# L3 attention: one product of 256 columns for the turned exponentials of two heads

## The chip, the cores and the metric

The kernel runs on one core of one Trainium2 chip. The metric is the time of one execution on the device in microseconds (us). Five engines work side by side, each through its own queue in order: TensorE (PE) multiplies matrices, VectorE (DVE) and ScalarE (ACT) read what PE leaves in PSUM, GpSimd (POOL) works on SBUF, and SyncE (SP) issues most of the transfers (DMA).

## The reference

The network has eight layers on 2048 tokens of 128 features, each of the form `x = layernorm(x + f(x))`: four pairs of an attention-like layer and a feed-forward layer, L0 to L3. The change touches only the attention of L3, which is this, cut to its core:

```python
NUM_HEADS, NUM_KV_HEADS, HEAD_DIM = 16, 4, 64
qkv = hidden_states @ qkv_w.T + qkv_b            # one sequence of 2048 tokens
xq, xk, xv = jnp.split(qkv, [H * D, H * D + KV * D], axis=-1)
xq = xq * scale                                  # scale from softplus(scaling), one per feature
xk = jnp.repeat(xk, 4, axis=2)                   # four query heads share one key head
xv = jnp.repeat(xv, 4, axis=2)
probs = jax.nn.softmax(jnp.einsum('bqhd,bkhd->bhqk', xq, xk))
out = jnp.einsum('bhqk,bkhd->bqhd', probs, xv)
return out.reshape(B, S, H * D) @ o_w.T + o_b
```

Every query sees all 2048 keys; there is no mask. All values are float32.

## The kernel before

Method `l3a` works on the attention of L3. The 2048 tokens are four blocks of 512 (`NB`), and each block is four tiles `t` of 128 queries. Of the four query heads of a key head `g`, two make a step: `groups` lists (block, tile, key head), each group gives two steps `s`, so there are 128 steps. The queries of a step's two heads are in the tile `qT` (64 features each), and a copy with the halves exchanged is in `qx`, made by two transfers of SP.

One of the two heads of a step goes the "A" way, the other the "B" way.

The A way has queries on the partitions. `scores_a(s, c)` (L1561) makes the scores of 128 queries against 1024 keys, in two halves c; DVE takes the maximum (`nm`, L1565), ACT the exponential with its sum (`e`, L1571); PE turns the result (`turn_a`, L1581), so that keys are on the partitions; ACT copies it out of PSUM (`et`, L1583); and `mixed_a` (L1593) multiplies it with the values `v`: 16 products of 128 columns, over 8 slices of keys in each of the two halves. A product's output has 64 partitions, so the two halves of the keys go side by side into the upper and the lower 64 partitions of `po`. ACT copies `po` to `pos` (L1602). Later the two halves are turned back (`divided`, L1630), scaled and added (`divided2`, L1635 and L1641), turned again (`turned`, L1645) and copied to `oA` (`turned2`, L1649).

The B way packs scores so that 32 queries lie on a quarter of the partitions and the four quarters hold four parts of the keys. `scores_b(s, x)` (L1677) makes them for two of the four groups of 32 queries at a time; DVE takes maxima (`st`, L1684), ACT exponentials (`eb`, L1692); statistics of the four parts are exchanged through DRAM by five transfers of SP (L1704, L1706) and joined (`joined1` to `joined3`, L1711 to L1729); POOL multiplies `eb` by the factors (L1732); DVE turns it in blocks of 32x32 (`turn_b`, L1739, `etb`); `mixed_b` (L1750) multiplies it with `v`, again 16 products of 128 columns; and DVE copies the result to `oB` (L1757).

At the end of each block, `out1` to `out5` multiply `oA` and `oB` with the output weights (L1763), add the input, normalize, and turn the result for the next layer.

The order on PE, DVE and ACT is written out by hand in `step(s)`; POOL's is left to the scheduler. A step computes scores and exponentials of `s + 1`, turns the A exponentials of `s`, and multiplies older ones with `v`: `mixed_a(s - 1)` in its first half, `mixed_b(s - 2)` in its second. `last(s)` closes it with the small products: queries for `s + 3` (L1537, `queries2` scales them on DVE, L1544), and one of `divided` and `turned`, in turn. Even and odd steps differ in these: one group is two steps, and what is made once per group (`factors1`, L1610, `factors3`, L1623, and the copy to `oA`) falls into one or the other.

What ties the engines together are few buffers. The scores and the turned A exponentials share the PSUM tile `s`, which has three buffers, taken in the order: A scores, turned A exponentials, B scores, and the same again in the second half of the step. `po` has one buffer, as has `tp`, which `last`, `out1`, `out2` and `out5` share:

```python
tc.tile_pool(name="l3a_s", bufs=3, space=PSUM) as ps,
tc.tile_pool(name="l3a_o", bufs=1, space=PSUM) as pso,
...
net.ps_t = shared.enter_context(tc.tile_pool(name=f"ps_t{len(net.coming)}", bufs=n, space=PSUM))
```

(`n` is 1 for `l3a`.)

Of the kernel before, what the change touches and what calls it, by code (L numbers as in the profile page):

```python
# [18 lines left out]
NB = NT // TB  # L19
NTILE = NT // 128  # L20
# [189 lines left out]
class _Net:  # L210
# [1254 lines left out]
    def l3a(self, xT, x_new):  # L1465
        nc, tc = self.nc, self.tc
        w = self.weights("w_l3a")
        wo = w[:, 1024:2560].rearrange("p (k m) -> p k m", k=12)
        rows = (slice(0, 64), slice(64, 128))
        with (  # L1470
# [14 lines left out]
            v = self.tile(one, [128, NTILE, 256], "v")  # L1485
            chunks = kT.rearrange("p x g (j m k) -> p x g j m k", m=NB, k=32)
            for b in range(NB):
                for g in (0, 1):
                    p = self.tile(ps, [128, 2, 512], "s")[:, 0, :]
                    nc.tensor.matmul(  # L1490
                        p,
                        lhsT=self.kv[:, g * 128 : (g + 1) * 128],
                        rhs=xT[:, b * TB : (b + 1) * TB],
                        start=True,
                        stop=True,
# [13 lines left out]
            oB = self.tile(one, [128, 8, 512], "oB")  # L1509
# [14 lines left out]
                    nc.vector.tensor_add(v[:, j, :], p[:, 0:256], self.bv)  # L1524


            groups = [(b, t, g) for b in range(NB) for t in range(4) for g in range(4)]
            n = 2 * len(groups)
            q_of, nm_of, den_of, e_of, et_of, po_of, pos_of, rec_of, ot_of, oT_of = ({} for _ in range(10))
            st_of, f_of, eb_of, etb_of, pob_of, r_of = ({} for _ in range(6))  # L1530

            def queries(s, p):

                b, t, g = groups[s // 2]
                c = 2 * g + s % 2
                at = b * TB + t * 128
                nc.tensor.matmul(  # L1537
                    p, lhsT=w[:, c * 128 : (c + 1) * 128], rhs=xT[:, at : at + 128], start=True, stop=True
                )
# [27 lines left out]

            def exponentials_a(s, c):
                k, h = divmod(s, 2)
                e = self.tile(sb, [128, 1024], "e", bufs=3)  # L1570
                nc.scalar.activation(  # L1571
                    e, e_of[s, c], AF.Exp, bias=nm_of[k][:, h, c : c + 1], accum_out=den_of[k][:, h, c : c + 1]
                )
                e_of[s, c] = e

            def turn_a(s, c):
                e = e_of.pop((s, c))
                tp = self.tile(ps, [128, 2, 512], "s").rearrange("p i (j q) -> p i j q", j=8)
                for j in range(8):
                    for i, r in enumerate(rows):  # L1580
                        nc.tensor.transpose(tp[:, i, j, :], e[r, j * 128 : (j + 1) * 128], self.ident[r, r])  # L1581
                et = self.tile(sb, [128, 2, 8, 64], f"et{c}", bufs=2 - c)
                nc.scalar.copy(et, tp)  # L1583
                et_of[s, c] = et

            def mixed_a(s):
                k, h = divmod(s, 2)
                g = groups[k][2]
                po = self.tile(pso, [128, 128], "po")
                ets = [et_of.pop((s, c)) for c in (0, 1)]  # L1590
                for j in range(8):
                    for c, r in enumerate(rows):
                        nc.tensor.matmul(  # L1593
                            po[r, :].rearrange("p (i q) -> p i q", i=2),
                            lhsT=v[:, 8 * c + j, g * 64 : (g + 1) * 64],
                            rhs=ets[c][:, :, j, :],
                            start=j == 0,
                            stop=j == 7,
                        )
                if h == 0:  # L1600
                    pos_of[k] = self.tile(sb, [128, 2, 128], "pos")
                nc.scalar.copy(pos_of[k][:, h, :], po)  # L1602


            wide = lambda x: x.unsqueeze(2).to_broadcast([128, 2, 2])
# [21 lines left out]
            def divided(k, tp):  # L1627
                pos = pos_of.pop(k)
                for h in range(2):
                    nc.tensor.transpose(tp[:, h, :], pos[:, h, :], self.ident)  # L1630
                ot_of[k] = tp
# [12 lines left out]
            def turned(k, tp):  # L1644
                nc.tensor.transpose(tp, ot_of.pop(k).rearrange("p h d -> p (h d)"), self.ident)  # L1645

            def turned2(k, tp):
                b, t, g = groups[k]
                nc.vector.tensor_copy(oA[:, g, t * 128 : (t + 1) * 128], tp)  # L1649

            def last(s):

                tp = self.tile(self.ps_t, [128, 4, 128], "tp")
                k, h = divmod(s - 2, 2)
                some = 0 <= k < len(groups)
                if some and h:
                    turned(k, tp[:, 1])
                if have(s + 3):
                    queries(s + 3, tp[:, 0])
                if some and not h:  # L1660
                    divided(k, tp[:, 1:3])
                if some and h:
                    turned2(k, tp[:, 1])
                if have(s + 3):
                    queries2(s + 3, tp[:, 0])
# [68 lines left out]
                    )  # L1734

            def turn_b(s, x):
                if x == 0:
                    etb_of[s] = self.tile(sb, [128, 4, 512], "etb")
                nc.vector.transpose(  # L1739
                    etb_of[s][:, 2 * x : 2 * x + 2, :].rearrange("p i k -> p (i k)"),  # L1740
                    eb_of.pop((s, x)).rearrange("p i k -> p (i k)"),
                )

            def mixed_b(s):
                b, t, g = groups[s // 2]
                po = self.tile(pso, [128, 128], "po")
                et = etb_of.pop(s)
                for j in range(NTILE):
                    r = rows[j % 2]
                    nc.tensor.matmul(  # L1750
                        po[r, :].rearrange("p (i q) -> p i q", i=4),
                        lhsT=v[:, j, g * 64 : (g + 1) * 64],
                        rhs=et[:, :, 32 * j : 32 * j + 32],
                        start=j < 2,
                        stop=j >= NTILE - 2,
                    )
                nc.vector.tensor_copy(oB[:, 2 * g + s % 2, t * 128 : (t + 1) * 128], po)  # L1757


            def out1(b):  # L1760
# [26 lines left out]
            have = lambda s: 0 <= s < n  # L1787

            def late(f, s, by, odd):

                k, h = divmod(s - by, 2)
                if h == odd and 0 <= k < len(groups):
                    f(k)

            def ends(f, s, by):

                if (s - by) % 32 == 31 and have(s - by):
                    f((s - by) // 32)

            def step(s):  # L1800
                new = have(s + 1)
                if new:
                    scores_a(s + 1, 0)
                if have(s):
                    turn_a(s, 0)
                if have(s - 1):
                    joined3(s - 1)
                late(factors1, s, 0, 1)
                if new:
                    exponentials_a(s + 1, 0)  # L1810
                    scores_b(s + 1, 0)
                ends(out1, s, 3)
                if s < 1:
                    values(range(8 * s + 8, 8 * s + 16))
                if new:
                    exponentials_b(s + 1, 0)
                if have(s - 2):
                    turn_b(s - 2, 1)
                late(divided2, s, 3, 0)
                if have(s - 1):  # L1820
                    mixed_a(s - 1)
                ends(out2, s, 4)
                if new:
                    scores_a(s + 1, 1)
                ends(out3, s, 4)
                if have(s):
                    turn_a(s, 1)
                late(factors2, s, 0, 1)
                if new:
                    exponentials_a(s + 1, 1)  # L1830
                    scores_b(s + 1, 1)
                late(factors3, s, 1, 1)
                if have(s):
                    joined1(s)
                if have(s - 1):
                    turn_b(s - 1, 0)
                ends(out4, s, 4)
                if new:
                    exponentials_b(s + 1, 1)
                if have(s):  # L1840
                    joined2(s)
                if have(s - 2):
                    mixed_b(s - 2)
                ends(out5, s, 4)
                last(s)

            with tc.manual_schedule(engines=MAIN - {mybir.EngineType.Pool}):
                keys_over(0)
                for s in (0, 1):
                    tp = self.tile(self.ps_t, [128, 4, 128], "tp")  # L1850
# [73 lines left out]
```

## Time and profile before

| what | value |
|---|---|
| three runs | 2726.64 us (median), 2713.97 to 2731.01 |
| the profiled execution | 2722.66 us, span 2720.8 us, mean granted TensorE clock 0.941 |
| busy: PE, DVE, ACT, POOL | 2446.3, 1801.6, 1481.7, 1165.3 us |
| first and last B-scores product (L1677) | start at 1258.9 and 2527.3 us |
| L1593 and L1750, PE | x4096 each, 276 ns mean, 252.0 and 251.9 us busy |
| L1739, DVE | x256, 1234 ns mean, 316.0 us busy |
| L1757, DVE | x128, 253 ns mean, 32.4 us busy |
| L1602, ACT | x128, 263 ns mean, 33.6 us busy |

The time of the run holds the span, from the first to the last instruction in the trace, and a little around it. Attention of L3 takes nearly half of the span. A float32 product shows as two matmul instructions, so 16 products are 32 of them (4096 = 128 x 32). Matmuls that follow each other overlap, so the mean of one (276 ns) is more than the time that it adds.

### The profile page before, as it was taken

Reading aid. Unit: us, or ns where it says so; the run is one execution under the profiler, and the core shown is the slowest. Engines: PE = TensorE matmul, PEld = TensorE weight load, DVE = VectorE, ACT = ScalarE, POOL = GpSimd, SP = SyncE. Lnnn points to the kernel's source line nnn. Section 1 sums busy time; section 2 is a strip of 40 time slices with the busy share of each in tenths; the row PEclk is TensorE's granted clock in tenths of the full one; section 3 lists DMA queues with packets and bytes.
Section 4 is the critical chain, followed back from the end, with each engine's and each line's share of the span. In section 5 each row is a group of like instructions: output and inputs, shape, how many; then the busy total and the mean of one; then the engine's idle time right before and its main releaser. Section 6 shows DMA issues by size and latency. Waiting matters only on the chain.

```text
span 2720.8 us, 59820 instructions
## 1 busy us (share of the span) xinstructions
PE 2446.3 (90%) x23773; PEld 1440.0 (53%) x23818; DVE 1801.6 (66%) x3156; ACT 1481.7 (54%) x2874; POOL 1165.3 (43%) x1403
## 2 busy tenths in 40 slices
PE   5779837998987888877999999999999999999998
PEld 3456524442224555543666656666566665666543
DVE  5443334013887777755888878888688887888311
ACT  1113312223435666644777757777577776777322
POOL 2142162003667776641555435554345553455200
PEclk8569957997998999998999999999999999999999
DMA  3011110000002111202000000000000000000000
GB/s 152 5 66 37 28 31 6 0 1 28 9 16 64 36 34 31 73 3 56 12 11 11 11 9 11 11 11 11 8 12 12 11 11 8 11 12 12 2 8 8
DMA packets 138923, 60.63 MB, mean 22 GB/s; under 512 B 100700, under 2 KB 130340, under 8 KB 137108
## 3 DMA queue, kind: packets, MB, share of 16 engines
q1 hardware_dynamic: 135942, 50.12, 8.0%
q0 software_dynamic: 2272, 4.66, 0.7%
q8 instruction: 190, 3.11, 0.5%
q10 hardware_dynamic: 432, 2.04, 0.2%
q14 instruction: 87, 0.70, 0.1%
HBM read 31.85 MB, written 5.23 MB: 14 GB/s over the span
## 4 chain that ended last, share of the span: by engine, by line
PE 76%; DVE 9%; ACT 6%; POOL 4%; issue 3%; DMA 1%; SPq 0%; POOLq 0%; DVEq 0%; ACTq 0%
PE s L1561 10%; PE s L1677 9%; PE po L1593 9%; PE po L1750 9%; PE mm L862 8%; PE s L1581 4%; PE h L673 3%; PE tp L1763 2%; PE tp L1537 1%; PE tp L703 1%; PE tp L1341 1%; DVE h L1068 1%; PE num L408 1%; PE mm L873 1%; PE mm L851 1%
## 5 line engine op out<-in xcount | busy, mean ns | idle before, releaser
L1732 POOL TENSOR_TENSOR eb<-eb,fb 128x1024 f32<-128x1024 f32 x256 | 479.5, 1894 | 5.0
L1583 ACT COPY et<-s 128x1024 f32<-128x1024 f32 x256 | 259.3, 1013 | 222.1 <-PE s L1581 221.9
L1692 ACT ACTIVATE eb<-s,st 128x512 f32<-128x512 f32 x512 | 347.0, 682 | 58.5 <-DVE st L1684 53.7
L1565 DVE TENSOR_REDUCE nm<-s 128x1 f32<-128x1024 f32 x256 | 313.3, 1224 | 87.1 <-PE s L1561 86.1
L1684 DVE TENSOR_REDUCE st<-s 128x2 f32<-128x1024 f32 x256 | 313.3, 1224 | 56.4 <-PE s L1677 49.5
L1739 DVE STREAM_TRANSPOSE etb<-eb 128x1024 f32<-128x1024 f32 x256 | 316.0, 1234 | 1.1 <-POOL eb L1732 0.9
L1561 PE MATMUL s<-kT,qx 64*128 64x512 f32 x512 | 290.9, 648 | 4.4 <-DMA qx<-qT 4.4
L1571 ACT ACTIVATE e<-s,nm 128x1024 f32<-128x1024 f32 x256 | 285.8, 1116 | 14.1 <-DVE nm L1565 13.7
L1561 PE MATMUL s<-kT,qT 64*128 64x512 f32 x512 | 290.0, 647 | 0.0
L1677 PE MATMUL s<-kT,qx 64*32 64x512 f32 x2048 | 279.2, 605 | 2.4 <-ACT eb L1692 2.4
L1677 PE MATMUL s<-kT,qT 64*32 64x512 f32 x2048 | 279.2, 605 | 0.0
L1593 PEld LDWEIGHTS po<-et,v 128*64 128x64 f32 x4096 | 221.1, 137 | 107.6 <-DVE db L1726 98.9
L1750 PEld LDWEIGHTS po<-etb,v 128*64 128x64 f32 x4096 | 221.0, 137 | 107.0 <-issue 106.3
L1750 PE MATMUL po<-etb,v 128*64 128x128 f32 x4096 | 251.9, 276 | 1.7 <-DVE etb L1739 1.3
L1593 PE MATMUL po<-et,v 128*64 128x128 f32 x4096 | 252.0, 276 | 0.7 <-DVE oB L1757 0.7
L1581 PEld LDWEIGHTS s<-ident,e 64*128 64x128 f32 x4096 | 170.2, 139 | 135.0 <-issue 103.8
L862 PE MATMUL mm<-h,wb 128*128 128x512 f32 x512 | 221.0, 592 | 0.0
L1581 PE MATMUL s<-ident,e 64*128 64x64 f32 x4096 | 169.8, 223 | 0.1
L297 POOL TENSOR_SCALAR ln_rs<-ln_mv 128x4 f32<-128x4 f32 x40 | 10.5, 262 | 365.8 <-DVE ln_mv L291 328.3
L875 DVE SCALAR_TENSOR_TENSOR r<-mm,vec,xT 128x512 f32<-128x512 f32 x8 | 6.0, 751 | 240.4 <-PE mm L873 240.4
L862 PEld LDWEIGHTS mm<-h,wb 128*128 128x128 f32 x512 | 97.3, 190 | 122.5 <-issue 119.8
L1729 POOL TENSOR_TENSOR fb<-dm,db 128x4 f32<-128x4 f32 x128 | 25.8, 202 | 259.6 <-DVE db L1727 132.8
(375 smaller groups left out, 4591.5 us busy)
## 6 DMA issues: line engine op xcount, KB each, us to landing
qx<-qT SPq DMA_DIRECT2D x256, 32.0 KB, 1.9
st<-std SPq DMA_DIRECT2D x512, 4.0 KB, 1.8
vo<-v SPq DMA_DIRECT2D x62, 128.0 KB, 2.4
ex<-in_w_ex_dram SPq DMA_DIRECT2D x4, 1536.0 KB, 16.9
rot<-in_rot_dram SPq DMA_DIRECT2D x32, 128.0 KB, 2.2
wb<-in_w_l1f_dram SPq DMA_DIRECT2D x1, 2816.0 KB, 9.5
wb<-in_w_l3f_dram SPq DMA_DIRECT2D x1, 2816.0 KB, 9.9
yd<-ys SPq DMA_DIRECT2D x39, 64.0 KB, 1.5
```

Source lines behind the costliest of these rows:

```text
L862: nc.tensor.matmul(p, lhsT=hid[i][:, k, c * 128 : (c + 1) * 128], rhs=h[:, k, :], start=k == 0, stop=k == 3,)
L1561: nc.tensor.matmul(p[:, i, :], lhsT=q_of[s][i][r, :], rhs=kT[r, (g + i) % 2, g // 2, at : at + 512], start=True, stop=True)
L1565: nc.vector.tensor_reduce(nm_of[k][:, h, c : c + 1], p, AX.X, ALU.max, negate=True)
L1571: nc.scalar.activation(e, e_of[s, c], AF.Exp, bias=nm_of[k][:, h, c : c + 1], accum_out=den_of[k][:, h, c : c + 1])
L1581: nc.tensor.transpose(tp[:, i, j, :], e[r, j * 128 : (j + 1) * 128], self.ident[r, r])
L1593: nc.tensor.matmul(po[r, :].rearrange("p (i q) -> p i q", i=2), lhsT=v[:, 8 * c + j, g * 64 : (g + 1) * 64], rhs=ets[c][:, :, j, :], start ...
L1677: nc.tensor.matmul(p[32 * m : 32 * m + 32, i, :], lhsT=q_of[s][1 - i][r, at : at + 32], rhs=chunks[r, (g + i) % 2, g // 2, :, m, :], start ...
L1684: nc.vector.tensor_reduce(st_of[s][:, 4, 2 * x : 2 * x + 2], p, AX.X, ALU.max, negate=True)
L1692: nc.scalar.activation(e[:, i, :], eb_of[s, x][:, i, :], AF.Exp, bias=st[:, 4, at : at + 1], accum_out=st[:, 4, 4 + at : 5 + at],)
L1732: nc.gpsimd.tensor_mul(e, e, f[:, 2 * x : 2 * x + 2].unsqueeze(2).to_broadcast([128, 2, 512]))
L1739: nc.vector.transpose(etb_of[s][:, 2 * x : 2 * x + 2, :].rearrange("p i k -> p (i k)"), eb_of.pop((s, x)).rearrange("p i k -> p (i k)"),)
L1750: nc.tensor.matmul(po[r, :].rearrange("p (i q) -> p i q", i=4), lhsT=v[:, j, g * 64 : (g + 1) * 64], rhs=et[:, :, 32 * j : 32 * j + 32], s ...
```

## The change

The A exponentials of step s and the B exponentials of step s - 1 are put into one tile `et` of shape [128, 2, 2, 4, 256]: half of the keys, A or B, group of 32 queries, and keys. `turn_a` writes its part in that order (PE's transposes now write two runs of 32 instead of one of 64, ACT's copy stays 1024 in a row), and `turn_b` writes the other part, in runs of 256. `mixed(s, part)` multiplies both with the same slice of `v` in one product of 256 columns, half of the 16 products in each half of the step. This needs both heads to belong to the same key head, so `groups` now runs over tiles inside of a key head; where the key head changes (15 times, and at both ends) `mixed` makes separate products of 128 columns as before. `copied` then copies both parts of `po` on ACT, at the end of the step: to `pos` and to `oB`. Both calls of `turn_b` for a step now stand together in the second half of the next one; before, one stood there and the other in the first half of the step after. `divided2`, and the work in `last` on the A part, come a step later; `out1` moves from the first half of its step to its end. The tile `e` has two buffers instead of three, `et` two of 16 KB per partition instead of the separate `et0`, `et1` and `etb`.

```diff
--- before.py
+++ after.py
@@ -1524,7 +1524,7 @@
                     nc.vector.tensor_add(v[:, j, :], p[:, 0:256], self.bv)
 
 
-            groups = [(b, t, g) for b in range(NB) for t in range(4) for g in range(4)]
+            groups = [(b, t, g) for b in range(NB) for g in range(4) for t in range(4)]
             n = 2 * len(groups)
             q_of, nm_of, den_of, e_of, et_of, po_of, pos_of, rec_of, ot_of, oT_of = ({} for _ in range(10))
             st_of, f_of, eb_of, etb_of, pob_of, r_of = ({} for _ in range(6))
@@ -1567,7 +1567,7 @@
 
             def exponentials_a(s, c):
                 k, h = divmod(s, 2)
-                e = self.tile(sb, [128, 1024], "e", bufs=3)
+                e = self.tile(sb, [128, 1024], "e")
                 nc.scalar.activation(
                     e, e_of[s, c], AF.Exp, bias=nm_of[k][:, h, c : c + 1], accum_out=den_of[k][:, h, c : c + 1]
                 )
@@ -1575,31 +1575,51 @@
 
             def turn_a(s, c):
                 e = e_of.pop((s, c))
-                tp = self.tile(ps, [128, 2, 512], "s").rearrange("p i (j q) -> p i j q", j=8)
+                tp = self.tile(ps, [128, 2, 512], "s").rearrange("p i (h j q) -> p i h j q", h=2, j=8)
                 for j in range(8):
                     for i, r in enumerate(rows):
-                        nc.tensor.transpose(tp[:, i, j, :], e[r, j * 128 : (j + 1) * 128], self.ident[r, r])
-                et = self.tile(sb, [128, 2, 8, 64], f"et{c}", bufs=2 - c)
-                nc.scalar.copy(et, tp)
-                et_of[s, c] = et
-
-            def mixed_a(s):
-                k, h = divmod(s, 2)
-                g = groups[k][2]
-                po = self.tile(pso, [128, 128], "po")
-                ets = [et_of.pop((s, c)) for c in (0, 1)]
-                for j in range(8):
+                        nc.tensor.transpose(tp[:, i, :, j, :], e[r, j * 128 : (j + 1) * 128], self.ident[r, r])
+                if c == 0:
+                    et_of[s] = self.tile(sb, [128, 2, 2, 4, 256], "et")
+                nc.scalar.copy(et_of[s][:, c, 0], tp.rearrange("p i h j q -> p (i h) (j q)"))
+
+            def mixed(s, part):
+
+                ga, gb = (groups[x // 2][2] if have(x) else None for x in (s, s - 1))
+                if part == 0:
+                    po_of[s] = self.tile(pso, [128, 8, 32], "po")
+                po, et = po_of[s], et_of[s]
+                if ga == gb:
+                    g, lo, hi, of = ga, 0, 8, range(4 * part, 4 * part + 4)
+                else:
+
+                    g, lo, hi, of = (gb, 4, 8, range(8)) if part else (ga, 0, 4, range(8))
+                if g is None:
+                    return
+                for j in of:
                     for c, r in enumerate(rows):
                         nc.tensor.matmul(
-                            po[r, :].rearrange("p (i q) -> p i q", i=2),
+                            po[r, lo:hi, :],
                             lhsT=v[:, 8 * c + j, g * 64 : (g + 1) * 64],
-                            rhs=ets[c][:, :, j, :],
+                            rhs=et[:, c].rearrange("p u i k -> p (u i) k")[:, lo:hi, 32 * j : 32 * j + 32],
                             start=j == 0,
                             stop=j == 7,
                         )
-                if h == 0:
-                    pos_of[k] = self.tile(sb, [128, 2, 128], "pos")
-                nc.scalar.copy(pos_of[k][:, h, :], po)
+
+            def copied(s):
+                po = po_of.pop(s)
+                et_of.pop(s)
+                if have(s):
+                    k, h = divmod(s, 2)
+                    if h == 0:
+                        pos_of[k] = self.tile(sb, [128, 2, 128], "pos")
+                    nc.scalar.copy(pos_of[k][:, h, :], po[:, 0:4, :].rearrange("p i q -> p (i q)"))
+                if have(s - 1):
+                    b, t, g = groups[(s - 1) // 2]
+                    nc.scalar.copy(
+                        oB[:, 2 * g + (s - 1) % 2, t * 128 : (t + 1) * 128],
+                        po[:, 4:8, :].rearrange("p i q -> p (i q)"),
+                    )
 
 
             wide = lambda x: x.unsqueeze(2).to_broadcast([128, 2, 2])
@@ -1651,7 +1671,7 @@
             def last(s):
 
                 tp = self.tile(self.ps_t, [128, 4, 128], "tp")
-                k, h = divmod(s - 2, 2)
+                k, h = divmod(s - 3, 2)
                 some = 0 <= k < len(groups)
                 if some and h:
                     turned(k, tp[:, 1])
@@ -1734,27 +1754,13 @@
                     )
 
             def turn_b(s, x):
-                if x == 0:
-                    etb_of[s] = self.tile(sb, [128, 4, 512], "etb")
+
+                if not have(s + 1) and x == 0:
+                    et_of[s + 1] = self.tile(sb, [128, 2, 2, 4, 256], "et")
                 nc.vector.transpose(
-                    etb_of[s][:, 2 * x : 2 * x + 2, :].rearrange("p i k -> p (i k)"),
-                    eb_of.pop((s, x)).rearrange("p i k -> p (i k)"),
+                    et_of[s + 1][:, :, 1, 2 * x : 2 * x + 2, :].rearrange("p c i k -> p i c k"),
+                    eb_of.pop((s, x)).rearrange("p i (c k) -> p i c k", c=2),
                 )
-
-            def mixed_b(s):
-                b, t, g = groups[s // 2]
-                po = self.tile(pso, [128, 128], "po")
-                et = etb_of.pop(s)
-                for j in range(NTILE):
-                    r = rows[j % 2]
-                    nc.tensor.matmul(
-                        po[r, :].rearrange("p (i q) -> p i q", i=4),
-                        lhsT=v[:, j, g * 64 : (g + 1) * 64],
-                        rhs=et[:, :, 32 * j : 32 * j + 32],
-                        start=j < 2,
-                        stop=j >= NTILE - 2,
-                    )
-                nc.vector.tensor_copy(oB[:, 2 * g + s % 2, t * 128 : (t + 1) * 128], po)
 
 
             def out1(b):
@@ -1799,6 +1805,7 @@
 
             def step(s):
                 new = have(s + 1)
+                pair = 0 <= s - 1 <= n
                 if new:
                     scores_a(s + 1, 0)
                 if have(s):
@@ -1809,16 +1816,13 @@
                 if new:
                     exponentials_a(s + 1, 0)
                     scores_b(s + 1, 0)
-                ends(out1, s, 3)
                 if s < 1:
                     values(range(8 * s + 8, 8 * s + 16))
                 if new:
                     exponentials_b(s + 1, 0)
-                if have(s - 2):
-                    turn_b(s - 2, 1)
-                late(divided2, s, 3, 0)
-                if have(s - 1):
-                    mixed_a(s - 1)
+                late(divided2, s, 4, 0)
+                if pair:
+                    mixed(s - 1, 0)
                 ends(out2, s, 4)
                 if new:
                     scores_a(s + 1, 1)
@@ -1834,15 +1838,19 @@
                     joined1(s)
                 if have(s - 1):
                     turn_b(s - 1, 0)
+                    turn_b(s - 1, 1)
                 ends(out4, s, 4)
                 if new:
                     exponentials_b(s + 1, 1)
                 if have(s):
                     joined2(s)
-                if have(s - 2):
-                    mixed_b(s - 2)
+                if pair:
+                    mixed(s - 1, 1)
                 ends(out5, s, 4)
                 last(s)
+                ends(out1, s, 3)
+                if pair:
+                    copied(s - 1)
 
             with tc.manual_schedule(engines=MAIN - {mybir.EngineType.Pool}):
                 keys_over(0)
```

## The prediction

> **What bounds the kernel now.** I read the page's busy shares and chain first, to see which engine sets the end, then its costliest groups, then the timeline of two steps of the L3 attention, for the slack of the other engines. (A bit over 1% is what a measurement of this kernel can tell from no change: the three runs lie 0.6% apart.)
>
> ```profile
> span 2720.8 us, 59820 instructions
> PE 2446.3 (90%) x23773; PEld 1440.0 (53%) x23818; DVE 1801.6 (66%) x3156; ACT 1481.7 (54%) x2874; POOL 1165.3 (43%) x1403
> ...
> PE 76%; DVE 9%; ACT 6%; POOL 4%; issue 3%; DMA 1%; SPq 0%; POOLq 0%; DVEq 0%; ACTq 0%
> ...
> L1565 DVE TENSOR_REDUCE nm<-s 128x1 f32<-128x1024 f32 x256 | 313.3, 1224 | 87.1 <-PE s L1561 86.1
> L1739 DVE STREAM_TRANSPOSE etb<-eb 128x1024 f32<-128x1024 f32 x256 | 316.0, 1234 | 1.1 <-POOL eb L1732 0.9 <-POOL f L1625 0.2
> ```
>
> PE is the chain. DVE waits for PE (86.1 us in front of L1565), so in this stage PE leads. But the lead is short: by the windows, 2000 to 2200 us has PE busy 200.00, DVE 178.97, ACT 156.90 of 200 us. The timeline shows how the three hang together. These are rows of one odd step, which begins at 2000.09:
>
> ```profile
> 2000.09 0.69 PE L1561 MATMUL s<-kT,qT 64*128 64x512 f32 x1
> ...
> 2001.30 1.23 DVE L1565 TENSOR_REDUCE nm<-s 128x1 f32<-128x1024 f32 x1 [0.20 <-PE s L1561]
> 2002.44 0.17 DVE L1726 TENSOR_REDUCE db<-dn 128x4 f32<-128x16 f32 x1
> ...
> 2002.74 0.13 DVE L1610 TENSOR_REDUCE m<-nm 128x2 f32<-128x4 f32 x1
> 2002.90 1.23 DVE L1684 TENSOR_REDUCE st<-s 128x2 f32<-128x1024 f32 x1
> ...
> 2004.04 1.23 DVE L1739 STREAM_TRANSPOSE etb<-eb 128x1024 f32<-128x1024 f32 x1
> 2004.16 0.69 ACT L1692 ACTIVATE eb<-s,st 128x512 f32<-128x512 f32 x1 [0.29 <-DVE st L1684]
> ...
> 2005.41 0.20 ACT L1692 ACTIVATION_READ_ACCUMULATOR eb<-s,st 128x1 f32 x1
> ...
> 2006.11 0.61 PE L1677 MATMUL s<-kT,qx 64*32 64x512 f32 x1
> ...
> 2007.31 1.22 DVE L1684 TENSOR_REDUCE st<-s 128x2 f32<-128x1024 f32 x1 [0.34 <-PE s L1677]
> 2008.45 0.17 DVE L1711 TENSOR_REDUCE mn<-st 128x4 f32<-128x16 f32 x1
> 2008.53 1.23 DVE L1739 STREAM_TRANSPOSE etb<-eb 128x1024 f32<-128x1024 f32 x1
> 2009.69 0.25 DVE L1757 COPY oB<-po 128x128 f32<-128x128 f32 x1
> ```
>
> See the two turns: one stands behind the first `st` maximum (2004.04), where DVE would otherwise wait for PE; the other behind the second (2008.53). See also the ring: PSUM tile `s` has three buffers, so the second B-scores product (2006.11) needs the exponentials of the first (read ends 2005.61): 0.50 us of slack.
>
> Steps begin at 1990.52, 2000.09, 2009.51, 2019.08: 9.57 for an even, 9.42 for an odd one, 18.99 for a pair, 64 pairs.
>
> **The change, part by part.**
>
> *Joint product.* By the chain, a half step of PE is 1.06 (L1561) + 0.49 (L1581) + 1.02 (L1677) + 1.90 (L1593 or L1750, 16 pairs of matmuls of 128 columns, 0.119 a pair); `last` adds 0.63 or 0.48. A pair of 256 columns isn't in this stage. Bounds: no gain, 0.238, so 8 pairs take 1.90; the rate of the 512-column pass (2000.63 to 2001.06, 0.43, so 0.215), 1.72. I take the line through 128 (0.119) and 512 (0.43), 0.223, so 1.78: a half step is 4.35, a step 8.70 + 0.63 = 9.33 or 9.18. PE alone would give 18.51 a pair, 0.48 less. Loads of weights halve, hidden under the matmuls already. At 15 changes of key head the 32 products stay as they were: 0.24 back each, half of it on the path, 2 us in all.
>
> The Trainium skill's "TensorE: Matmul & The Clock Gate", section "Back-to-back issue gap", gives less: 134 cycles for 128 columns and 262 for 256, so two products become one for 2.2%; by that estimate a half step keeps 1.86 and the forecast would be 8 us higher.
>
> *Where the turns go.* Both turns of the step now stand behind the second `st` maximum and `mn`. Queued behind them on DVE: `oA`, `qT` and the next step's `nm`, for which ACT's exponentials wait, and then PE. So I add up the way from one second B-scores product to the next, start to start:
> - product to `st`: 2006.11 to 2007.31, 1.20
> - `st` to the turn: 1.22 (odd step), 1.61 in an even one (1997.76 to 1999.37, with `s` and its reciprocal)
> - two turns: each 1.16 (2008.53 to 2009.69), 2.32
> - `oA`, now in the even step, 0.20 (2009.87 to 2010.07); `qT` 0.31 (0.39 less the 0.08 by which DVE's next operation starts early)
> - `nm` to `st`: 1.60 in an odd step (2001.30 to 2002.90), 1.44 in an even one (no `m`, 0.16)
> - `st` to the exponential: 2002.90 to 2004.16, 1.26
> - exponentials to PE: 1.45 to the end of the read, and 0.05 until PE takes the buffer, as in the only place where it waited for it, the stage's start:
>
> ```profile
> 1270.56 0.20 ACT L1692 ACTIVATION_READ_ACCUMULATOR eb<-s,st 128x1 f32 x1
> ...
> 1270.82 0.61 PE L1677 MATMUL s<-kT,qx 64*32 64x512 f32 x1 [0.66 <-ACT eb L1692]
> ```
>
> Out of an even step into an odd: 1.20 + 1.61 + 2.32 + 0.20 + 0.31 + 1.60 + 1.26 + 1.50 = 10.00. Out of an odd into an even: 1.20 + 1.22 + 2.32 + 0.31 + 1.44 + 1.26 + 1.50 = 9.25. Before, with one turn here and `oB`'s 0.18, the longer is 8.82: hidden under PE's 9.42. After, PE needs 9.33 out of an odd step and 9.18 out of an even one, so the pair is 10.00 + 9.33 = 19.33: 0.34 more than 18.99. Times 64: 22 us. So the stall goes from nowhere to PE, in front of the B-scores product, and the moved turn costs more than the product saves.
>
> *The copy of the B part* goes from DVE (0.25, L1757; 0.18 of its queue) to ACT, with `pos` moved to the step's end: 0.36 of ACT's queue, under the 1.05 to 1.18 us that ACT waits for PE in front of L1583; if that cover went, 0.36 a step. It waits for the product's second part, over before ACT arrives. `po` is free 1 us before its next use.
>
> *At nothing:* the new shape of L1581's output (same 64 columns) and the copy from it (1024 in a row); the third buffer of `e` (its reader L1581 is done before ACT writes again); order of groups (same tiles). POOL's products (2003.20 to 2006.94) end before both turns. No DMA is added; `qT`, and so the `qx` transfers on SP, are about 1 us later, used two steps on. The turns end 5.2 us after the second B-scores product, the joint product begins at 5.8: 0.6 of slack, else PE waits there too.
>
> *The turn's output is now strided* (runs of 256). Bounds: nothing, since `kT`'s strided write costs 751 ns (L1500) against 749 for whole rows (L952); at most 12%, the costliest operation of 128x1024 on DVE (L364, 1388 ns) against 1234. I take nothing, the row that differs in stride alone.
>
> *Ends of blocks.* `out1` (24 matmuls, 10.2 us) now follows `last` at once, shares its one buffer `tp`, and so waits for `qT`, queued behind both turns: DVE gets there 1.20 + 1.61 + 2.32 + 0.20 + 0.40 = 5.73 after the product, PE 1.02 + 1.78 + 0.48 = 3.28: 2.4 us of PE, less 0.4 which the next step saves because DVE has caught up. Three times 2.0, 6 us (bounds 0 and 10). The last block's `divided2` and turn come a step later, with nothing beside them: 1 to 3, I take 2.
>
> Sum: 22 + 2 + 6 + 2 = 32 us on a profiled execution of 2722.7 us (span 2720.8), 4 us under the median 2726.64 of the runs: 2755.
>
> *The clock.* After PE's idle of 2.59 and 0.77 us at 1626 the granted clock was 0.61 from 1628 to 1632; from 2530 to 2545, with PE busy 12.02 of 15.00 and gaps up to 1.34, it was 1.00. The new gaps are 0.8 us (10.00 less 9.18) in every other step: I charge nothing.
>
> The same page of the Trainium skill, section "A second HAM failure mode: psum-queue depth-cycling", speaks against this: short idles between groups that cycle PSUM buffers made the clock swing between half and full; if a tenth of PE's work ran at half rate, my estimate is some 70 us more, and no row here shows it.
>
> **The rivals.**
> 1. PE still sets the pace (faster). One mechanism: the round trip over DVE and ACT is shorter than summed. For: DVE is busy only 8.4 of a step and the sum joins latencies of separate rows. Against: each term is a back-to-back spacing. It breaks even at 9.66 instead of 10.00 and is all gained at 9.18: 64 x 0.48 = 31 less, plus 10 for changes and ends: 2702.
> 2. About level: `s` is free when the second exponential ends, not its read (0.15 less), and ends of blocks cost nothing: 64 x 0.19 + 4 = 16, 2739. Against: the 1270.82 row.
> 3. The strided turn costs the 12%: 0.145 x 4 turns, of which 0.29 + 0.21 lie on the pair: 32 more, 2787.
> 4. The change doesn't do what it says: the 256-column products run at no gain. Then PE needs 9.57 out of an odd step: 19.57, 15 more, 2770.
>
> **How the numbers follow.** Forecast 0.48, own range 2740 to 2772; rival 1 0.12, rival 2 0.20, rival 3 0.12, rival 4 0.08. Slower by over 1% starts at +27: four fifths of the forecast, rivals 3 and 4, less a little for doubt of the block ends: 0.56. Within 1%: the rest and rival 2, 0.32. Faster: rival 1, since ends and changes leave nothing of its lower half within: 0.12. The range goes from just above rival 1's full gain, 2708, to rival 3 with block ends at their bound and some more, 2806.
>
> **What would show it.** In the profile after: steps of about 9.9 and 9.3 in turn, or 19.3 a pair; PE idle of some 50 us (64 x 0.8) in front of the B-scores product, put down to ACT `eb`; DVE's idle in front of the first `nm` gone and new idle behind the first `st`; the turn still at 1234 ns; matmuls of 256 columns at some 380 ns; ACT with 33 us more, DVE 32 less. Wrong if the pair is under 18.99, if the idle is in front of the joint product instead, or if the turn's mean moves.

## The result, and the profile after

The changed kernel takes 2759.20 us (median of 8 runs, 2749.41 to 2767.69) against 2724.58 us (8 runs) before: ratio 1.0121, with a 95% interval of 1.0099 to 1.0143, so about 33 us more. The prediction said 2755 and "slower by over 1%".

The profiled execution is the longest of the eight (2767.69 us). Of its excess, 12 us lie in front of the changed stage, in layers that the change doesn't touch: the first B-scores product starts at 1270.8 us, before at 1258.9. (In the eleven profiled executions of this record it starts anywhere from 1248.4 to 1271.4.) So I read the stage by itself, from the start of the first B-scores product to the start of the last: 1268.4 us before (1258.9 to 2527.3), 1300.2 after (1270.8 to 2571.0), 31.8 more. From there to the end of the span it is 193.5 before and 194.9 after, 1.4 more.

First the page of the changed kernel: busy time, chain, and the groups that were shown of before.

```profile
span 2765.9 us, 52811 instructions
...
PE 2475.2 (89%) x20234; PEld 1301.3 (47%) x20234; DVE 1753.2 (63%) x3028; ACT 1509.4 (55%) x3002; POOL 1164.3 (42%) x1403
...
PE 58%; DVE 24%; ACT 9%; POOL 4%; issue 4%; DMA 1%; DVEq 0%; SPq 0%; POOLq 0%; ACTq 0%
...
L1565 DVE TENSOR_REDUCE nm<-s 128x1 f32<-128x1024 f32 x256 | 312.4, 1220 | 140.5 <-PE s L1561 140.5
...
L1760 DVE STREAM_TRANSPOSE et<-eb 128x1024 f32<-128x1024 f32 x256 | 302.4, 1219 | 2.5 <-POOL eb L1752 2.3
L1697 PE MATMUL s<-kT,qx 64*32 64x512 f32 x2048 | 278.5, 603 | 23.3 <-ACT eb L1712 23.3
```

PE's share of the chain fell from 76% to 58%, and DVE's rose from 9% to 24%, although every engine's share of the span is about as before. That is the sign to look for: no engine is fuller, but the chain now runs over three of them. The turn itself costs no more than before (1219 ns against 1234).

The chain of waits in order of time, from 2050 to 2070 us, shows which way it goes (start, duration, what):

```profile
2049.88 2.36 DVE et L1760 x2
2052.24 0.18 DVE oA L1669
2052.41 0.32 DVE qT L1544
2052.73 1.13 DVE nm L1565
...
2054.20 1.14 DVE st L1704
...
2055.37 1.46 ACT eb L1712 x4
2056.82 0.04 issue
2056.87 1.09 PE s L1697 x16
2057.96 1.88 PE po L1601 x16
...
2060.47 1.06 PE s L1561 x4
...
2067.60 1.23 DVE st L1704
...
2069.20 1.23 DVE et L1760
```

Out of an even step (its turns begin at 2049.88) the chain is the round trip of the prediction: two turns, `oA`, `qT`, the next step's `nm` and `st`, the exponentials, and only then PE's second B-scores product. Out of the odd step that follows it is PE alone, until the next even step's second maximum at 2067.60. The timeline has the single waits:

```profile
2048.27 1.23 DVE L1704 TENSOR_REDUCE st<-s 128x2 f32<-128x1024 f32 x1 [0.34 <-PE s L1697]
...
2052.64 1.22 DVE L1565 TENSOR_REDUCE nm<-s 128x1 f32<-128x1024 f32 x1
...
2054.11 1.22 DVE L1704 TENSOR_REDUCE st<-s 128x2 f32<-128x1024 f32 x1
...
2056.61 0.20 ACT L1712 ACTIVATION_READ_ACCUMULATOR eb<-s,st 128x1 f32 x1
...
2056.87 0.61 PE L1697 MATMUL s<-kT,qx 64*32 64x512 f32 x1 [0.34 <-ACT eb L1712]
...
2058.09 1.23 DVE L1704 TENSOR_REDUCE st<-s 128x2 f32<-128x1024 f32 x1 [0.79 <-PE s L1697]
```

From one second maximum to the next it is 9.82 us here (2048.27 to 2058.09) and 9.51 to the one after (2067.60): 19.33 a pair of steps, where it was 18.99. PE took the buffer 0.06 us after the end of the read (2056.81), as in the row that the prediction went by.

### The profile page after: what moved, and what is told of

Same layout as the page of the kernel before. It is cut to its first block, busy times and chain, and to the rows that moved or that the text cites. A ratio compares the mean times of both kernels' runs of the same rounds, so it can differ in the third digit from the quotient of the medians.

```text
span 2765.9 us, 52811 instructions
## 1 busy us (share of the span) xinstructions
PE 2475.2 (89%) x20234; PEld 1301.3 (47%) x20234; DVE 1753.2 (63%) x3028; ACT 1509.4 (55%) x3002; POOL 1164.3 (42%) x1403
## 4 chain that ended last, share of the span: by engine, by line
PE 58%; DVE 24%; ACT 9%; POOL 4%; issue 4%; DMA 1%; DVEq 0%; SPq 0%; POOLq 0%; ACTq 0%
PE po L1601 8%; PE mm L862 8%; PE s L1697 7%; DVE et L1760 6%; DVE st L1704 5%; PE s L1561 5%; ACT eb L1712 3%; DVE nm L1565 3%; PE h L673 2%; PE s L1581 2%; PE tp L1769 2%; PE tp L703 1%; PE tp L1341 1%; DVE h L1068 1%; PE num L408 1%
## 5 line engine op out<-in xcount | busy, mean ns | idle before, releaser
L1601 PE MATMUL po<-et,v 128*64 128x256 f32 (+1 forms) x4608 | 499.0, 361 | 3.2 <-ACT et L1584 1.4
L1601 PEld LDWEIGHTS po<-et,v 128*64 128x64 f32 x4608 | 293.4, 136 | 311.0 <-issue 209.5
L1760 DVE STREAM_TRANSPOSE et<-eb 128x1024 f32<-128x1024 f32 x256 | 302.4, 1219 | 2.5 <-POOL eb L1752 2.3
L1697 PE MATMUL s<-kT,qx 64*32 64x512 f32 x2048 | 278.5, 603 | 23.3 <-ACT eb L1712 23.3
L869 ACT ACTIVATE h<-mm,vec 128x512 f32<-128x512 f32 x64 | 44.0, 687 | 157.2 <-PE mm L862 157.2
L1561 PEld LDWEIGHTS s<-kT,qT 64*128 64x128 f32 x512 | 76.0, 186 | 65.8 <-issue 41.4
```

Source lines behind the costliest of these rows:

```text
L1561: nc.tensor.matmul(p[:, i, :], lhsT=q_of[s][i][r, :], rhs=kT[r, (g + i) % 2, g // 2, at : at + 512], start=True, stop=True)
L1601: nc.tensor.matmul(po[r, lo:hi, :], lhsT=v[:, 8 * c + j, g * 64 : (g + 1) * 64], rhs=et[:, c].rearrange("p u i k -> p (u i) k")[:, lo:hi, ...
L1697: nc.tensor.matmul(p[32 * m : 32 * m + 32, i, :], lhsT=q_of[s][1 - i][r, at : at + 32], rhs=chunks[r, (g + i) % 2, g // 2, :, m, :], start ...
L1760: nc.vector.transpose(et_of[s + 1][:, :, 1, 2 * x : 2 * x + 2, :].rearrange("p c i k -> p i c k"), eb_of.pop((s, x)).rearrange("p i (c k) ...
```

## The experiments

Two theories. A: the place of the turns, both behind the second B maximum, makes the round trip from PE over DVE and ACT back to PE the pace; the joint product is worth little, and the ends of blocks cost some more. B: the joint product and its tiles cost the time, and the turns' place is free.

| kernel | pair of steps, us | stage, us | ratio to before, 95% interval |
|---|---|---|---|
| before | 18.99 | 1268.4 | 1 |
| changed | 19.33 | 1300.2 | 1.0121 (1.0099 to 1.0143) |
| e1: before, turns together | 19.38 | 1294.6 | 1.0118 (1.0086 to 1.0149) |
| e2: changed, split products | 19.36 | 1301.0 | 1.0145 (1.0113 to 1.0176) |
| e3: changed, one turn between the maxima | 18.90 | 1275.1 | 1.0034 (1.0017 to 1.0051) |
| e5: e3, split products | 18.99 | 1275.9 | 1.0031 (1.0006 to 1.0057) |
| e4: e3, `out1` in a buffer of `s` | 18.91 | 1264.8 | 0.9998 (0.9983 to 1.0014) |
| e6: changed, `out1` in a buffer of `s` | 19.32 | 1290.0 | 1.0107 (1.0077 to 1.0136) |
| e7: e4, scaling in front of the turn | 18.91 | 1263.6 | 0.9971 (0.9947 to 0.9995) |
| e8: e7, split products | 18.99 | 1262.7 | 0.9999 (0.9972 to 1.0026) |
| e9: changed, second turn made twice | 21.53 | 1444.3 | one run, 2895.13 us |

Pair and stage are from one profiled execution each, the ratio from all runs. The pair is the same, within 0.06 us, nearly everywhere in the stage but at its start and at the three ends of blocks that lie in it.

**e1, the turns' place alone.**

```diff
-                if have(s - 2):
-                    turn_b(s - 2, 1)
...
                     turn_b(s - 1, 0)
+                    turn_b(s - 1, 1)
```

> The kernel before, with the products as they were; only the second turn of the B part moves, from behind the first B maximum of the next step to behind the first turn. Theory A (the turns' place makes the round trip from PE over DVE and ACT back to PE the pace): the trip out of an even step into an odd one is 9.81 us (as in the trace of the changed kernel, where oB's copy and oA's have changed places) against PE's 9.57, out of an odd into an even 9.53 against 9.42: the pair of steps is 19.34 instead of 18.99, 22 us more, about 2746, ratio 1.008; PE waits for ACT's eb in front of the second B-scores product. Theory B (the joint product and its strided tiles cost the time, the turns' place nothing): 2724, ratio 1.000, no such wait.

Measured: 2754.27 us, ratio 1.0118. Moving one DVE instruction, with the products and `out1` as they were, makes a loss as large as the whole change. The pair is 19.38, close to theory A's 19.34, and its 0.39 makes 25 of the 26 us by which the stage is longer (0.39 x 64; 22 were expected). At the ends of blocks little is lost here: PE's waits for the normalized rows (`ln_xn`, L304) grew from 7.8 us to 11.1, but those for `ot` (L1635) fell from 3.3 to 2.0.

**e3, one turn elsewhere.** The first turn goes between the second A maximum and the second B maximum:

```diff
                 ends(out3, s, 4)
+                if have(s - 1):
+                    turn_b(s - 1, 0)
...
-                    turn_b(s - 1, 0)
                     turn_b(s - 1, 1)
```

> The changed kernel, with the first of the two turns taken out of the queue behind the second B maximum and put between the second A maximum and the second B maximum of the same step, where DVE waited 0.34 to 0.79 us for PE. Theory A: the round trip is now 9.81 less 1.14 (the turn) plus 0.72 (the second B maximum starts late by what of the turn goes beyond DVE's wait), 9.39, just under PE's own way out of an even step (9.38), so PE sets the pace again with 18.9 us a pair; what is left of the loss is the block ends and the group changes, 5 to 10 us: 2728, ratio 1.001. Theory B: stays at 2759, ratio 1.012.

Measured: 2732.41 us, ratio 1.0034, 0.9% under the changed kernel, with a pair of 18.90. The waits of PE in the stage (who waited for whom, total, times, longest):

```profile
PE tp L312 <- DVE ln_xn L304: 11.2, 3, 3.7
PE tp L1769 <- DVE qT L1544: 5.5, 3, 1.8
PE s L1697 <- ACT eb L1712: 3.4, 4, 1.6
```

The wait for `eb` was 23.3 us in 63 places; it is gone but for the stage's start and ends. What is left are ends of blocks. Theory B falls: joint product and tiles are all in here.

**e9, the dose.** A third turn behind the second maximum:

```diff
-                nc.vector.transpose(
...
+                for _ in range(1 + x):
+                    nc.vector.transpose(
```

> The changed kernel with the second turn made twice, so that one more operation of 1.14 us stands behind the second B maximum; the result stays as it is. Theory A: both ways are now over DVE and ACT: out of an even step 9.81 + 1.14 = 10.95, out of an odd one 1.20 + 1.23 + 2.28 + 0.29 + 1.43 + 1.24 + 1.50 = 9.17, and 1.14 more, 10.31, over PE's 9.52. The pair is 21.26 instead of 19.33, 124 us more: 2883. If DVE's queue behind the second maximum were not on the round trip, DVE has 1.6 us a step left (8.4 of 200 us slices of 10 us busy) and nothing would change: 2759.

Measured, in one execution: a pair of 21.53 (expected 21.26), a stage 144 us longer than the changed kernel's (expected 124), though DVE had 3.17 us of each 19.33 idle (busy 16.16). PE's waits in the stage:

```profile
PE s L1697 <- ACT eb L1712: 100.1, 121, 0.9
PE po L1601 <- DVE et L1762: 29.8, 47, 2.7
```

Now PE waits for `eb` in nearly every step. The rest is a second wait: the joint product itself comes before its turns are done. The prediction gave that 0.6 us of slack; an operation of 1.14 us goes beyond it.

**e2 and e5, what the joint product is worth.** Both make products of 128 columns in every step (`if ga == gb and s < 0`), e2 in the changed kernel, e5 in e3, where PE sets the pace.

> The changed kernel, both turns behind the second B maximum as it has them, but with separate products of 128 columns in every step. Theory A: the round trip still sets the way out of an even step (9.81 us), and out of an odd one PE needs 0.05 us more (9.57 instead of 9.52): 3 us in all, 2762, ratio 1.013. If the joint product were worth what the prediction took (0.24 us a step), the odd steps alone would be 15 us longer: 2774, ratio 1.018.

> As the one with the turn between the maxima, but every step makes separate products of 128 columns, as at a change of the key head: 32 instead of 16 in a step. With PE setting the pace, this measures what the joint product is worth. If it's what the traces show (a half step's products 1.88 us joint, 1.90 split): 0.04 us a step, 5 us in all, 2733, ratio 1.003. If it's what the prediction took (1.78 joint): 0.24 a step, some 27 us more than with the joint product, ratio 1.011.

Measured: e2 2762.92 us, 1.0145, e5 2730.15 us, 1.0031. The pair is 0.03 longer in e2 and 0.09 in e5, so the joint product is worth at most 6 us (0.09 x 64) where PE sets the pace, and not the 27 that the prediction's price would make. In time the pairs of kernels can't be told apart: the intervals overlap, and e5's stage is only 0.8 us longer than e3's. What hides the gain there is the clock at the ends of blocks. Here are the first products of `out1` at the first end, e3 and then e5 (start, duration, what, and in brackets PE's wait before):

```profile
1596.59 5.40 PE L1769 MATMUL tp<-oA,ws 128*128 128x512 f32 x8 [1.84 <-DVE qT L1544]
1598.45 3.70 PE L1769 MATMUL tp<-oA,ws 128*128 128x512 f32 x8 [1.82 <-DVE qT L1544]
```

After the same wait they took 1.7 us more in e3: the granted clock was 0.50 there for 3.4 us, at the first and the third of the three ends, and in e5 it was 1.00 at these places. Two times 1.7 is 3.4 of the 5 us.

**e4 and e6, the ends of blocks.** `out1` takes a buffer of `s`, and multiplies `oB` first:

```diff
-                y = self.tile(self.ps_t, [128, 512], "tp")
-                for c in range(12):
+                y = self.tile(ps, [128, 2, 512], "s")[:, 0, :]
+                for c in (4, 5, 6, 7, 8, 9, 10, 11, 0, 1, 2, 3):
```

> As the one with the turn between the maxima, and out1 takes a buffer of the tile s instead of the single tp and multiplies the eight parts of oB before the four of oA, so it needn't wait for qT and oA behind the turns. The trace of the changed kernel has PE waiting 2.3 us for qT there, three times, 7 us in all. Theory A: 5 to 7 us below the one without it, 2722, ratio 0.999. If the block ends have other reasons than this wait (the queue of DVE in front of the normalization): no change from the one without.

> The changed kernel with out1 in a buffer of the tile s and the parts of oB first, both turns left behind the second B maximum. Theory A with the block ends as a cost of their own: the three waits of 2.3 us for qT go, 7 us, and two of the stretches at half clock that follow them (3.4 us each), 3 us more: 10 us below the changed kernel, 2749, ratio 1.009. If the round trip were all of the loss: no change, 1.012.

Measured: e4 2723.56 us, 0.9998; e6 2753.65 us, 1.0107. In the stage the edit takes 10.3 us off e3 and 10.2 off the changed kernel, the 10 expected of e6 and more than the 5 to 7 expected of e4; in time e4 lies below e3 and the intervals don't meet, while e6 is below the changed kernel, but within its interval. The traces account for e6's 10: PE's 6.8 us of waiting for `qT` are gone, and so are two stretches of 3.4 us at a granted clock of 0.50 behind these waits (at 1622.4 and 1953.5 in the changed kernel), 3.4 us at full rate. So the loss has two parts: some 22 us of round trip (0.34 x 64) and 10 of ends.

**e7 and e8, a version that might be below both.** e7 moves `ends(out4, s, 4)` in front of the second turn; e8 is e7 with split products.

> As the one with the turn between the maxima and out1 in a buffer of s, and at a block's end the scaling of the normalized rows (out4) stands in front of the second turn in DVE's queue, not behind it. PE's wait for it, 3.7 us three times, falls to about 2.5 or less, if POOL has the root by then: 4 us, and 3 to 10 us more where the stretch at half clock (6.8 us each) that follows goes with it: 2715 to 2720, ratio 0.996 to 0.998, a little below both kernels. If POOL's root is what it waits for: no change, 1.000.

> As the one with the scaling first, but with separate products of 128 columns in every step: the new order without the joint product. If the joint product is worth 0.02 us a half step as the traces show, the stage is 5 us longer than with it, and the time 2723, ratio 0.999; if the gain over the kernel before comes from the block ends alone and the product is worth nothing, 2718, ratio 0.997; if the product carries it (0.24 us a step), 30 us more.

Measured: e7 2718.33 us, 0.9971 (0.9947 to 0.9995), the only one of nine whose interval lies below 1, and barely; e8 2723.21 us, 0.9999. PE's wait for the scaled rows is 2.6 us at the longest instead of 3.7 (8.5 us in all, 11.9 in e4), but the stretches at a granted clock of 0.50 behind it stayed, 6.8 us at each of the three ends, and the stage is only 1.2 us below e4's, where 4 and more were expected. It is 4.8 us (0.2%) below the stage of the kernel before. Whether e7's 0.3% needs the joint product stays open in time: the two intervals overlap. The stages are level (1263.6 and 1262.7), but not because the product is worth nothing: the pair is 0.08 longer in e8 (5 us over 64), and against that the clock was 0.50 in e8 only for 3.4 us at two of the ends.

## Why the prediction was right, point by point

**The mechanism and the sum.** That the chain would run out of an even step over DVE and ACT back to PE, and out of an odd one over PE alone, is what the trace shows, and e1, e3 and e9 show that the turns' place makes it so. The forecast was a pair of 19.33 us, and it is 19.33, but to the hundredth that is luck: both ways were wrong, by the same amount in opposite directions. Out of an even step it had 10.00; the trace has 9.82. Out of an odd one it had 9.33; the trace has 9.51.

**The step that was too long: `nm` to `st`, 1.60.** After, it is 1.47 (2052.64 to 2054.11). The row that I took it from, 2001.30 to 2002.90, held a wait for PE that the timeline doesn't mark: `st` followed `m` by 0.16 there, with PE's last B-scores product ending at 2002.73, and by 0.04 once that product was ready early. The other terms hold within 0.04: `st` to the turns 1.61, the turns 2.28, `st` to the exponential 1.26, exponentials to PE 1.50.

**The step that was too short: the joint product, 1.78.** It is 1.88 (2057.96 to 2059.84 in the chain) against 1.90 for the split ones. The price came from a line between 0.119 for 128 columns and 0.43 for 512. But 0.119 is an average that has the start and the end of a run of products in it, and 0.43 is a spacing without them. Inside a run the pairs follow each other by 0.109 in the trace before (14 spacings, 2002.82 to 2004.35) and by 0.216 after (6 spacings, 2063.24 to 2064.54): twice 0.109 less 0.002. In both, the first pair takes 0.05 more than that (0.16 and 0.27), and from the start of the last to the next kind of matmul it is 0.10 more (0.21 and 0.32); so 16 x 0.109 + 0.15 is 1.90, and 8 x 0.216 + 0.15 is 1.88. There is almost nothing per instruction to save. The Trainium skill's "TensorE: Matmul & The Clock Gate", section "Back-to-back issue gap", has this for an isolated product, a time in proportion to the columns and 2.5 ns, and the estimate from it was 1.86 (the section's figures for a stream of products, less than twice the time for four times the columns, are not borne out here). That formula was nearer than my line, and rival 4 (no gain) was true; its own 2770 missed because it kept the 10.00.

**The ends of blocks.** PE's wait for `qT` in front of `out1` was put at 2.4 us, and is 2.3, three times. The prediction charged 8 us for the ends and the tail; e6 shows 10 for `out1` alone. What it left out is, first, that the normalized rows wait behind both turns too (PE's waits for them grew from 7.8 us to 11.2), though the waits for `ot`, 3.3 us before, are gone in return; and second, the clock. It looked only at the gaps inside steps, which cost nothing, as it said (from 1300 to 1590 us the granted clock is 1.00 in both kernels). At the ends of blocks, the stretches around `out1` and the normalization, it fell. Columns: window, length, busy time and count of PE, PEld, DVE, ACT and POOL, granted clock, DMA share, GB/s; before first, then the changed kernel.

```profile
1590.00:1660.00 70.00, 65.54 (x809) 40.14 (x801) 49.42 (x88) 41.37 (x93) 26.68 (x41) 0.98 0.06 8
1910.00:1990.00 80.00, 75.54 (x937) 45.94 (x933) 57.77 (x100) 49.14 (x110) 33.18 (x49) 0.96 0.06 9
2225.00:2320.00 95.00, 90.54 (x1176) 55.92 (x1164) 71.67 (x123) 61.53 (x135) 40.23 (x59) 0.98 0.07 9
```

```profile
1590.00:1660.00 70.00, 63.01 (x606) 32.62 (x604) 43.82 (x75) 38.80 (x89) 25.43 (x36) 0.93 0.06 8
1910.00:1990.00 80.00, 72.65 (x717) 37.31 (x709) 52.08 (x89) 46.89 (x107) 30.90 (x46) 0.94 0.06 8
2225.00:2320.00 95.00, 87.00 (x905) 44.82 (x901) 65.22 (x109) 58.77 (x135) 39.54 (x56) 0.96 0.06 9
```

The clock lost is 0.05 x 70 + 0.02 x 80 + 0.02 x 95 = 7 us at full rate, though not all of it need be on the path. So the sum had a term missing at the ends. Its two small terms were too long: where the key head changes the steps are some 0.02 us longer (9.53 instead of 9.51) and not 0.12 (half of the 0.24), so that 15 changes make less than half a us and not 2; and the tail is the 1.4 us above, not 2. The total, 32 against 33, came out because the short term at the ends and the long ones partly cancel.

The swing of the clock inside the steps, which the prediction held against itself, did not come. Its price was also not what it says: a tenth of the stage's work at half rate is some 127 us more (a tenth of 1268), and 70 fits a tenth of its time.

**What was costed at nothing** held: the strided turn (1219 ns; singly, in e3, 1236), and the copies on ACT, which still waits 0.70 to 0.84 us for PE before it copies the turned A exponentials. PE's idle in front of the B-scores product was put at 50 us and is 23 to 32 (by the matmul and by its load), because the two wrong terms had spread the ways further apart than they are: 10.00 against 9.18, where the traces have 9.82 against 9.38 (PE's own way out of an even step, in e3), which makes 28 us.

## What to carry to other kernels

Where a ring of few PSUM buffers ties three engines together, an engine that is busy 84% of the time (16.16 of 19.33 us) can set the pace without being full: add up the way from a buffer's fill to its next fill, start to start, over all engines and over two steps if they differ, and see what stands in the queue on that way before anything is moved into it. The same instruction is free behind the first maximum and costs 1% of the kernel behind the second. And take a price per instruction from the spacing inside a run of them, not from an average that has the run's start and end in it: merging products halves their number and leaves their columns.

## What the runs showed of the hardware

The clock after idle, in the changed kernel (columns as above):

```profile
1620.00:1626.00 6.00, 3.74 (x7) 1.70 (x7) 2.59 (x4) 1.10 (x6) 0.34 (x2) 0.72 0.09 9
1644.00:1655.00 11.00, 6.59 (x52) 3.47 (x50) 6.11 (x13) 3.83 (x10) 1.30 (x5) 0.69 0.07 9
```

With a wait of PE of 3.74 us, at 1644 to 1648, the granted clock had a mean of 0.69 from 1644 to 1655, and with one of 2.26 us in front of `out1` a mean of 0.72 from 1620 to 1626; the gaps of 0.3 to 0.5 us in every other step of the changed kernel left it at 1.00. I had expected the steps' gaps not to matter, and not that a wait of 2 to 4 us at three block ends would be paid a second time.

What the same wait costs differs from one time to the next. In the kernel before, PE waited 2.59 us for the normalized rows at each of the three ends, and the granted clock was 0.50 for 3.4, 6.8 and 3.4 us around it; in e8, with waits of 2.6 us, for 3.4 us, not at all, and 3.4. So a difference of a few us between two traces of this kernel can be the clock at the ends alone.

A float32 product of 256 columns took 0.216 us inside a run where one of 128 took 0.109: the merged instruction saved 1%.
